# A second level of block products in the second projection, with softmax, attention and normalisation moved to other stages

## Chip, cores, metric

One core of one Trainium2 chip. The metric is the device time of one execution in microseconds; a kernel's time is the median of its runs. Ratios are the mean time of one kernel's fast runs over the mean of the other's fast runs of the same rounds, so they are not quite the ratio of the medians printed beside them. Every experiment was timed against the kernel before on the same chip in the same rounds, and across experiments I compare ratios, as the chips differ a little.

## The reference, cut to what matters

Input x is 128 x 64 x 512, float32. One layer, added to x:

```python
h = relu(layernorm(x))
# first graph attention: H = 4 heads, each 512 -> 512
Wh  = einsum('bnf,hfo->bhno', h, W_heads)
e   = leaky_relu(f1 + f2), masked by adj;  attn = softmax(e)
h   = elu(attn @ Wh)                      # 4 heads side by side: 2048 columns
# second graph attention: one head, 2048 -> 512
Wh2 = h @ W_out
out = elu(softmax(scores(Wh2)) @ Wh2)
# feed-forward and final norm
y   = relu(out @ w1 + b1) @ w2 + b2 + out
x   = x + layernorm(y) * ln_gamma + ln_beta
```

The 8192 rows are worked off in 16 groups of 512 rows. "Second projection" is `h @ W_out`.

## The kernel before

Each 512 x 512 product is cut into 2 x 2 blocks and done with seven block products in place of eight (`unit`). A block product of the second projection is four float32 matmuls of 256 columns per head (`product_n`). Its seven results are combined while they leave PSUM, the memory that TensorE writes to (an *eviction* is such a step out of PSUM): one VectorE addition, some ScalarE copies.

```python
    def unit(name, product, post, order):
        own = {1: 1, 2: 1, 5: 5, 3: 5, 6: 6, 7: 6, 4: 6}   # the PSUM bank of each product
        def after(p):
            if p in (1, 5, 6):
                ...
                if p == 6:
                    nc.vector.tensor_tensor(gb[6], gb[6], sb["s1"], ALU.add)
                nc.scalar.copy(sb[nm], gb[p])
                post(nm, sb[nm])
            ...
    def product_n(ms, blocks):
        ...
                    w, a = piece(ms[i], p), blocks(p, i)      # 256 KB of weights
                    for k in range(2):
                        for j in range(2):
                            nc.tensor.matmul(bk[:, j, :], a[:, k, ts(j, P)], w[:, k, :], ...)
```

The final norm, a tile of 128 rows at a time, was placed in the second stage, between the feed-forward products:

```python
        def finish(j):
            t = G * g + j
            xr = load(t, "xr")
            nc.gpsimd.tensor_tensor(xr, xr, bs, ALU.add)
            y = o[:, j]
            mean, rstd = norm_stats(y, "n2", t)     # ends with a GpSimd power operation
            nc.vector.scalar_tensor_tensor(y, y, mean, gs, ALU.subtract, ALU.mult)
            nc.vector.scalar_tensor_tensor(y, y, rstd, xr, ALU.mult, ALU.add)
            nc.sync.dma_start(out=of[ts(t, P), :], in_=y)
```

A group has two stages. In the **head stage** the first projection runs (products g_a) with the second attention of the previous group beside it (`stage_e`: scores, softmax, transposes, attention). In the **second stage** the second projection runs (g_b), then the feed-forward of the previous group (g_c, g_d), with the first attention of later groups beside it.

Of the kernel before, what the change touches and what calls it, by code (L numbers as in the profile page):

```python
# [18 lines left out]
AHEAD = 150  # L19


@with_exitstack
def gat_preln_kernel(
# [63 lines left out]
    mhalf = const.tile([P, 1], FP, name="mhalf")  # L87
# [4 lines left out]
    def load(t, name="x"):  # L92

        tl = wk.tile([P, F], FP, tag="x", name=f"{name}{t}", bufs=4)
        nc.sync.dma_start(out=tl, in_=xf[ts(t, P), :])
        return tl
# [47 lines left out]
    MT, TC = {}, {}  # L144
    DIRECT = {}

    def fetch(m):
        MT[m] = big.tile([P, KC, O], FP, tag=homes[m], name=f"pw{m}")
        queue = nc.scalar if m < H else nc.gpsimd
        queue.dma_start(out=MT[m], in_=mats[m].rearrange("(k p) o -> p k o", p=P))  # L150
# [13 lines left out]
    def turn_a():  # L164

        rows = H * 2 * KC
        pt = aux([P, rows], "pah")
        nc.tensor.transpose(pt, ah, ident[0:rows, 0:rows])
        aT = wk.tile([P, H, 2, KC], FP, tag="s1", name="aT")
        nc.scalar.copy(aT.rearrange("p h c o -> p (h c o)"), pt)  # L170
        return aT

    def fold_dve(m, ab):

        for k in range(KC):
            for c in range(2):
                junk = wk.tile([P, O], FP, tag="t", name=f"jk{c}_{m}_{k}")
# [21 lines left out]
    def weight_sums(m, after=None):  # L199
# [20 lines left out]
        TC[m] = [dram.tile([P, 2, 2, Q], FP, name=f"tc{m}_{i}") for i in range(2)]  # L220
# [19 lines left out]


    late = []
# [17 lines left out]
    def unit(name, product, post, order):  # L260
# [5 lines left out]
        def after(p):  # L266
            if p in (1, 5, 6):
                nm = {1: "s1", 5: "s5", 6: "t"}[p]
                sb[nm] = wk.tile([P, 2, T], FP, tag=nm, name=f"{nm}_{name}")
# [30 lines left out]
    def product_t(m, blocks):  # L300

        def product(p):
            def fn(bk, start):
                w, a = piece(m, p), blocks(p)
                for o in range(2):
                    for k in range(2):
                        nc.tensor.matmul(  # L307
# [6 lines left out]
    def product_n(ms, blocks):  # L314

        def product(p):
            def part(i):
                def fn(bk, start):
                    w, a = piece(ms[i], p), blocks(p, i)
                    for k in range(2):  # L320
                        for j in range(2):
                            nc.tensor.matmul(  # L322
# [17 lines left out]
    def norm_stats(src, tag, t):  # L340

        st = sm.tile([P, 6], FP, tag=tag + "st", name=f"{tag}st{t}")
        nc.vector.bn_stats(st, src)
        mv = sm.tile([P, 2], FP, tag=tag + "mv", name=f"{tag}mv{t}")
        nc.vector.bn_aggr(mv, st)
        ve = sm.tile([P, 1], FP, tag=tag + "ve", name=f"{tag}ve{t}")
        nc.vector.tensor_scalar(ve, mv[:, 1:2], EPS, None, ALU.add)  # L347
        rstd = sm.tile([P, 1], FP, tag=tag + "rs", name=f"{tag}rs{t}")
        nc.gpsimd.tensor_tensor(rstd, ve, mhalf, ALU.pow)
        return mv[:, 0:1], rstd  # L350

    def norm1(t):
        if t not in X:
            X[t] = load(t)
        mean, rstd = norm_stats(X[t], "n1", t)
        nb = sm.tile([P, 1], FP, tag="n1nb", name=f"n1nb{t}")
        nc.gpsimd.tensor_scalar(nb, mean, rstd, -1.0, ALU.mult, ALU.mult)
        HN[t] = big.tile([P, F], FP, tag="hn", name=f"hn{t}", bufs=G)
        nc.scalar.activation(HN[t], X.pop(t), AF.Relu, bias=nb, scale=rstd)
# [15 lines left out]
    def project_f(g):  # L375
# [15 lines left out]
        eng = nc.vector if g == 0 else nc.gpsimd  # L391
        eng.tensor_tensor(
# [65 lines left out]
    A1, E1, LAST = {}, {}, {}  # L458
# [4 lines left out]
    def transpose_weights(p):  # L463
        A = A1.pop(p)
        for j in range(2):
# [7 lines left out]
            AT[t] = big.tile([P, NB, H, N], FP, tag="at", name=f"at{t}", bufs=G)  # L473
# [6 lines left out]
    def stage_a(g):  # L480


        if g >= NG:
            return [], [], []
        p, r = 2 * g, 2 * g + 1

        def norms(p):
            norm1(2 * p)
            norm1(2 * p + 1)
            if p >= 2:  # L490
                prefetch(2 * p + 2)
                prefetch(2 * p + 3)

        def transposes(p):
# [3 lines left out]
        return (  # L498
            [lambda: norms(p), lambda: norms(r)],
            [  # L500
                lambda: transposes(p), lambda: transposes(r), nothing, lambda: project_f(g), nothing,
                lambda: (scores1(g), attn_weights(p)), nothing, lambda: attn_weights(r),
            ],
            [nothing, lambda: transpose_weights(p), nothing, nothing, lambda: transpose_weights(r)],
        )
# [4 lines left out]
    def attend1(g):  # L510
# [3 lines left out]
        def task(j, half):  # L514
# [6 lines left out]
            banks = [bank(f"pz{nm}_{t}_{b}") for b in range(NB)]  # L521
# [8 lines left out]
            for b in range(NB):  # L530
# [3 lines left out]
                if b == 0:  # L534
# [28 lines left out]
    def project1(g, h):  # L563
# [11 lines left out]
        def post(what, a, b=None, to=None):  # L575
# [8 lines left out]
            if what == "c21":  # L584
                nc.gpsimd.tensor_tensor(dst, dst, H1["22"][:, h], ALU.add)  # L585

# [15 lines left out]
    WH2 = {}  # L602

    def project2(g):
        slot = {1: "11", 2: "12", 3: "12", 4: "22", 5: "S1", 6: "11", 7: "S1"}
        h1 = dict(H1)
        wh = big.tile([P, G, FO], FP, tag="wh2", name=f"wh2_{g}")
        WH2[g] = wh

        def post(what, a, b=None, to=None):  # L610
            behind = {"s1": ("11", "S1", "11"), "s5": ("S1", "22", "11"), "c11": ("12", "12", "11")}
            if what in behind:
                dst, x0, x1 = (h1[n] for n in behind[what])
                for h in range(H):
                    nc.gpsimd.tensor_tensor(dst[:, h], x0[:, h], x1[:, h], ALU.subtract)  # L615
# [11 lines left out]
            f"b{g}", product_n(ms, lambda p, i: h1[slot[p]][:, i]), post, (1, 5, 6, 2, 7, 3, 4)  # L627
# [5 lines left out]
    def scores2(g, j):  # L633
# [3 lines left out]
        for c in range(2):  # L637
            junk = wk.tile([P, FO], FP, tag="elu", name=f"jf{g}_{j}_{c}", bufs=3)
            nc.vector.scalar_tensor_tensor(  # L639
                junk, WH2[g][:, j], 1.0, ao[:, c, :], ALU.mult, ALU.mult,  # L640
                accum_out=f[:, c, j:j + 1],
            )

# [27 lines left out]
    def attend2(g, j):  # L671
        pa = aux([P, FO], f"pa2_{g}_{j}")
        nc.tensor.matmul(pa, AT2[g][:, j, :], WH2[g][:, j, :], start=True, stop=True)  # L673
# [5 lines left out]
    def stage_e(g):  # L679

        gap = [lambda: None]
        score = [lambda j=j: scores2(g, j) for j in range(G)]
        attend = [lambda j=j: attend2(g, j) for j in range(G)]
        return (
            gap + score + [lambda: spread2(g)] + gap * 2 + [lambda: softmax2(g)] + gap * 5
            + [lambda: transpose_weights2(g)] + gap * 2 + attend[0:2] + gap + attend[2:4] + gap * 3
        )


    def feed_forward(g):  # L690
# [42 lines left out]
        def post2(what, a, b=None, to=None):  # L733
# [5 lines left out]
            eng = nc.vector if what[0] == "c" else nc.gpsimd  # L739
            eng.tensor_tensor(dst, a, dst, ALU.add)  # L740

        def finish(j):
            t = G * g + j
            xr = load(t, "xr")
            nc.gpsimd.tensor_tensor(xr, xr, bs, ALU.add)
            y = o[:, j]
            mean, rstd = norm_stats(y, "n2", t)
            nc.vector.scalar_tensor_tensor(y, y, mean, gs, ALU.subtract, ALU.mult)
            nc.vector.scalar_tensor_tensor(y, y, rstd, xr, ALU.mult, ALU.add)
            nc.sync.dma_start(out=of[ts(t, P), :], in_=y)  # L750

        f1 = unit(f"c{g}", product_t(M1, lambda p: bl[1][p]), post1, (1, 5, 6, 2, 3, 7, 4))
        f2 = unit(f"d{g}", product_n([M2], lambda p, i: bl[2][p]), post2, (1, 5, 6, 2, 3, 7, 4))
        return (
            [lambda j=j: transpose_out(j) for j in range(G)], f1 + f2,
            [lambda j=j: finish(j) for j in range(G)],
        )

    def mix(*lists):

        lists = [l for l in lists if l]
        keyed = [((i + 0.5) / len(l), n, fn) for n, l in enumerate(lists) for i, fn in enumerate(l)]
        return [fn for _, _, fn in sorted(keyed, key=lambda k: k[:2])]
# [4 lines left out]
    for t in range(G):  # L768
        norm1(t)
# [45 lines left out]
    for t in range(G, 2 * G):  # L815
        prefetch(t)
    for g in range(NG):
        if g >= 1:
            side = stage_e(g - 1)
        else:  # L820
            side = sum(stage_a(1), [])
# [73 lines left out]
```

## Time and profile before

| | kernel before |
|---|---|
| median of 3 runs | 2364.24 us (2363.18 to 2365.32) |
| profiled span | 2360.4 us |
| a steady group | 142.96 us |
| its head stage, first g_a to first g_b | 50.9 us |
| its second stage, from a full run of g_b to the next g_a | 89.2 us |
| TensorE busy | 98% |

The two stage lengths are worked out from start times in the TensorE timeline; a mixed stretch of some 3 us between them is in neither. I use them as "head" and "second".

The prediction shows the page's first lines and the steady stretches. What it does not show is TensorE's list of waits (columns: who waits for whom, us in total, times, longest). Its longest entries occur once each, in the start; two of them:

```profile
PE pzS L525 <- DVE z L537: 5.5, 1, 5.5
...
PE pab L158 <- DMA ar<-in_L_gnn_a_heads_dram: 5.4, 1, 5.4
```

Two VectorE groups by form, to be compared later (columns: busy us, mean ns of one, idle before it and what ended it). Both have two inputs in SBUF; the first is the score sum of the second attention, the second the last step of the final norm:

```profile
L639 DVE SCALAR_TENSOR_TENSOR jf<-wh,ao 128x512 f32<-128x512 f32 x128 | 94.3, 776 | 40.3 <-ACT wh L621 40.1
L749 DVE SCALAR_TENSOR_TENSOR o<-o,n2rs,xr 128x512 f32<-128x512 f32 x64 | 47.7, 767 | 0.8 <-POOL n2rs L349 0.8
```

### The profile page before, as it was taken

To read this page: it belongs to the slowest core of one execution; us is meant where nothing else is said; L and a number is where in the kernel's file an instruction comes from. 1 tells how busy PE (TensorE), PEld (TensorE's weight loads), DVE (VectorE), ACT (ScalarE), POOL (GpSimd) and SP (SyncE) were. 2 spreads that over 40 slices of the span, in tenths; PEclk is the share of its full clock that TensorE was granted. 3 is DMA by queue.
4 is the path that set the end of the run, shared out by engine and by line. 5 is a ranking of instruction groups with operands and counts; after the bars stand their busy time and mean duration, and the time that the engine had idled before them with its cause. 6 is when DMAs were issued, how large, how long until landed. Compare 5 with 4: busy or idle time off the path is not lost.

```text
span 2360.4 us, 32849 instructions
## 1 busy us (share of the span) xinstructions
PE 2317.9 (98%) x11805; PEld 1934.5 (82%) x11805; DVE 1265.5 (54%) x2210; ACT 911.0 (39%) x1623; POOL 1026.7 (43%) x917
## 2 busy tenths in 40 slices
PE   6989999999999999999999999999999999999997
PEld 4868787888878888787887878888788887878885
DVE  7625474554646556474554745556464563744527
ACT  2524425253352533425244251533525344251513
POOL 5664444416344353443524444253443534533333
PEclk7999999999999999999999999999999999999999
DMA  8545353444535445353444544435354453534443
GB/s 308 184 142 193 125 183 127 164 152 132 182 125 178 134 139 179 126 180 129 154 163 129 182 131 161 153 130 181 127 177 132 138 179 127 182 118 164 157 148 106
DMA packets 257809, 366.89 MB, mean 155 GB/s; under 512 B 22216, under 2 KB 145128, under 8 KB 257648
## 3 DMA queue, kind: packets, MB, share of 16 engines
q1 hardware_dynamic: 251024, 343.82, 43.9%
q0 software_dynamic: 4512, 16.78, 1.9%
q10 hardware_dynamic: 2112, 4.19, 0.5%
q8 instruction: 95, 1.56, 0.3%
q14 instruction: 66, 0.54, 0.1%
HBM read 337.45 MB, written 27.26 MB: 155 GB/s over the span
## 4 chain that ended last, share of the span: by engine, by line
PE 94%; DVE 2%; ACT 1%; POOL 1%; issue 0%; DMA 0%; DVEq 0%
PE g_b L322 33%; PE g_a L307 32%; PE g_c L307 8%; PE g_d L322 8%; PE pz L525 4%; PE pa L673 2%; PE pto L700 1%; PE pzS L525 1%; PE pth L371 1%; PE s1pt L472 1%; PE pf L381 1%; PE s1pe L406 1%; DMA x<-in_x_dram 0%; PE s2pt L667 0%; PE pwa L193 0%
## 5 line engine op out<-in xcount | busy, mean ns | idle before, releaser
L322 PE MATMUL g_b<-w,h 128*128 128x256 f32 x2560 | 598.1, 381 | 0.0
L322 PEld LDWEIGHTS g_b<-w,h 128*128 128x128 f32 x2560 | 480.5, 190 | 72.2 <-issue 10.1
L307 PE MATMUL g_a<-z,w 128*128 128x256 f32 x1520 | 361.0, 380 | 1.2 <-DVE g_a L581 0.7
L307 PE MATMUL g_a<-zs_z,w 128*128 128x256 f32 x1504 | 347.9, 379 | 0.0
L307 PEld LDWEIGHTS g_a<-z,w 128*128 128x128 f32 x1520 | 287.6, 190 | 57.9 <-issue 14.3
L307 PEld LDWEIGHTS g_a<-zs_z,w 128*128 128x128 f32 x1504 | 284.8, 190 | 50.5 <-issue 14.3
L322 PE MATMUL g_b<-w,hS 128*128 128x256 f32 x1024 | 243.5, 382 | 0.0
L585 POOL TENSOR_TENSOR hS<-hS,h 128x512 f32<-128x512 f32 x64 | 83.0, 1297 | 366.8 <-DVE hS L549 366.8
L547 ACT ACTIVATE exc<-g_a 128x512 f32<-128x512 f32 x256 | 152.3, 595 | 199.7 <-DVE g_a L581 119.6
L322 PEld LDWEIGHTS g_b<-w,hS 128*128 128x128 f32 x1024 | 191.4, 191 | 30.9 <-issue 6.7
L549 DVE SCALAR_TENSOR_TENSOR h<-exc,g_a 128x512 f32<-128x512 f32 x192 | 131.6, 686 | 136.3 <-ACT exc L548 136.2
L548 ACT ACTIVATE exc<-exc 128x512 f32<-128x512 f32 x256 | 161.6, 631 | 6.5
L615 POOL TENSOR_TENSOR h<-h,h 128x512 f32<-128x512 f32 x64 | 86.7, 1362 | 138.1 <-PE g_b L322 138.0
L332 POOL TENSOR_TENSOR zs_z<-zS,z 128x512 f32<-128x512 f32 x63 | 89.7, 1424 | 128.3 <-PE g_a L307 123.7
L615 POOL TENSOR_TENSOR h<-hS,h 128x512 f32<-128x512 f32 x64 | 81.1, 1268 | 142.4 <-PE g_b L322 142.4
L474 ACT COPY at<-s1pt 128x512 f32<-128x512 f32 x64 | 34.7, 588 | 279.8 <-PE s1pt L472 279.8
L307 PE MATMUL g_c<-ot,w 128*128 128x256 f32 x512 | 123.9, 385 | 0.8 <-DVE n2ve L347 0.8
L322 PE MATMUL g_d<-w,rt 128*128 128x256 f32 x512 | 121.5, 380 | 1.7 <-DVE o L740 1.0
L307 PE MATMUL g_a<-zS,w 128*128 128x256 f32 x496 | 117.2, 379 | 0.0
L639 DVE SCALAR_TENSOR_TENSOR jf<-wh,ao 128x512 f32<-128x512 f32 x128 | 94.3, 776 | 40.3 <-ACT wh L621 40.1
L333 POOL TENSOR_TENSOR zs_z<-z,zs_z 128x512 f32<-128x512 f32 x63 | 85.4, 1357 | 61.1 <-PE g_a L307 40.7
L307 PEld LDWEIGHTS g_c<-ot,w 128*128 128x128 f32 x512 | 93.9, 190 | 21.8 <-issue 9.3
(159 smaller groups left out, 3535.6 us busy)
## 6 DMA issues: line engine op xcount, KB each, us to landing
w<-tc SPq DMA_DIRECT2D x632, 256.0 KB, 2.6
w<-in_L_gnn_W_heads_dram SPq DMA_DIRECT2D x192, 256.0 KB, 2.7
w<-in_L_gnn_W_out_dram SPq DMA_DIRECT2D x192, 256.0 KB, 2.7
w<-in_L_gnn_w_dram SPq DMA_DIRECT2D x96, 256.0 KB, 2.7
x<-in_x_dram SPq DMA_DIRECT2D x66, 256.0 KB, 3.6
xr<-in_x_dram SPq DMA_DIRECT2D x64, 256.0 KB, 2.8
out_dram<-o SPq DMA_DIRECT2D x64, 256.0 KB, 2.1
tc<-pt POOLq DMA_DIRECT2D x20, 512.0 KB, 5.6
```

Of the source, the lines that this page charges most:

```text
L307: nc.tensor.matmul(bk[:, o, :], w[:, k, ts(o, P)], a[:, k, :], start=start and o == 0 and k == 0, stop=k == 1, skip_group_check=True,)
L322: nc.tensor.matmul(bk[:, j, :], a[:, k, ts(j, P)], w[:, k, :], start=start and k == 0 and j == 0, stop=i == len(ms) - 1 and k == 1, skip_g ...
L332: eng.tensor_tensor(s2, s1, a11, ALU.subtract)
L333: eng.tensor_tensor(s4, a12, s2, ALU.subtract)
L525: nc.tensor.matmul(banks[b][:, c, :].rearrange("p (h n) -> p h n", h=H), src[rows, off + c * P:off + (c + 1) * P], at[rows, b], start=True ...
L547: nc.scalar.activation(ex, src, AF.Relu, scale=-1.0)
L548: nc.scalar.activation(ex, ex, AF.Exp, scale=-1.0)
L549: nc.vector.scalar_tensor_tensor(dst, ex, -1.0, src, ALU.add, ALU.max)
L585: nc.gpsimd.tensor_tensor(dst, dst, H1["22"][:, h], ALU.add)
L615: nc.gpsimd.tensor_tensor(dst[:, h], x0[:, h], x1[:, h], ALU.subtract)
L639: nc.vector.scalar_tensor_tensor(junk, WH2[g][:, j], 1.0, ao[:, c, :], ALU.mult, ALU.mult, accum_out=f[:, c, j:j + 1],)
L673: nc.tensor.matmul(pa, AT2[g][:, j, :], WH2[g][:, j, :], start=True, stop=True)
```

## The change

The intent is to take work from TensorE: each of the seven products of the second projection is cut once more, into seven of quarter size (7 x 7 x 4 heads = 196 matmuls of 128 columns for 7 x 16 = 112 of 256). This runs in groups 4 to 15, the *deep* groups below; groups 1 to 4 prepare the summed weights. Softmax and first attention of the next group move into the second stage, half of the final norm moves on into the next head stage (`last`), and "not urgent" operations are tied behind the last issued matmul (`behind_pe`) so that they do not take their engine's place from an eviction. Its core:

```diff
+DEEP = 4
+    def behind_pe(ins):            # a dependency on the last issued matmul
+        if "pe" in LAST:
+            tc.add_manual_dep(ins.ins, LAST["pe"].ins.name, ...)
+    def project2_deep(g):
+        def quarter_sum(p, j):     # 21 a group, 128x512, two SBUF inputs
+            eng = nc.gpsimd if p in (3, 7, 4) else nc.vector
+            ...
+        def inner(r, eng):         # recombines the inner level: 5 operations, twice a group
+            behind_pe(eng.tensor_tensor(...)); eng.tensor_tensor(...) ...
+        def part(p, half, j):
+                w, x = small_piece(p, j), operand(p, j)
+                for h in range(H):
+                    LAST["pe"] = nc.tensor.matmul(bk[:, place[j][1]], x[:, h], w[:, h], ...)
+                ...
+                        if p == 7:
+                            inner(0, nc.gpsimd)
+                        if p == 4:
+                            inner(1, nc.gpsimd)
+        def fin_load(j):
+            xr[j] = load(t, "xr")
+            nc.gpsimd.tensor_tensor(xr[j], xr[j], bs, ALU.add)
+        def fin_stats(j, gate=True):      # two tiles at a time; one power operation
+        def fin_out(j, gate=True):        # the two scalar_tensor_tensor, then the output transfer
-            [lambda j=j: finish(j) for j in range(G)],
+            (fin_load, fin_stats, fin_out),
     # second stage of group g (a position is a share of the stage's steps):
+            tasks += [(0.60 + 0.08 * j, lambda j=j: fin_load(j)) for j in range(G)]
+            tasks += [(0.84, lambda: fin_stats(0))]
+            tasks += [(0.93 + 0.03 * j, lambda j=j: fin_out(j)) for j in range(2)]
     # head stage of group g + 1:
+            last = [(0.03, lambda f=fin_stats: f(2))]
+            last += [(0.09 + 0.03 * j, lambda j=j, f=fin_out: f(2 + j)) for j in range(2)]
     # second attention, in the head stage:
+            [(0.14 + 0.06 * j, lambda j=j: scores2(g, j)) for j in range(G)]
+            + [(0.36, lambda: spread2(g)), (0.44, lambda: softmax2(g))]
+            + [(0.64, lambda: transpose_weights2(g))]
+            + [(0.72 + 0.06 * j, lambda j=j: attend2(g, j)) for j in range(G)]
```

Also: buffers are taken from others to make room, and the copies of the first attention move from VectorE to ScalarE.

## The prediction

> **What bounds the kernel now.** I read the page first, then the busy time by stretch, the chain of waits in order of time, the groups by form, the TensorE timeline and the packet records. Page: span, busy time, chain.
>
> ```profile
> span 2360.4 us, 32849 instructions
> PE 2317.9 (98%) x11805; PEld 1934.5 (82%) x11805; DVE 1265.5 (54%) x2210; ACT 911.0 (39%) x1623; POOL 1026.7 (43%) x917
> ...
> PE 94%; DVE 2%; ACT 1%; POOL 1%; issue 0%; DMA 0%; DVEq 0%
> PE g_b L322 33%; PE g_a L307 32%; PE g_c L307 8%; PE g_d L322 8%; PE pz L525 4%; PE pa L673 2%; PE pto L700 1%; PE pzS L525 1%; PE pth L371 1%; PE s1pt L472 1%; PE pf L381 1%; PE s1pe L406 1%; DMA x<-in_x_dram 0%; PE s2pt L667 0%; PE pwa L1
> ```
>
> TensorE is busy for 98% and carries 94% of the chain. The stretches say the same for one steady group: head stage (products g_a), then second stage (g_b, the second projection, with g_c and g_d, the feed-forward, between). Columns: window, length, then busy us of each engine, granted clock, DMA share, GB/s.
>
> ```profile
> 1191.45:1242.21 50.76, 50.76 (x230) 43.21 (x230) 27.21 (x52) 28.31 (x51) 11.69 (x9) 1.00 0.45 148
> 1242.21:1334.41 92.20, 92.20 (x506) 76.51 (x505) 50.81 (x82) 28.40 (x51) 48.90 (x44) 1.00 0.46 151
> sum 142.96, PE 142.96 PEld 119.73 DVE 78.02 ACT 56.72 POOL 60.59; mean PE 71.48 PEld 59.86 DVE 39.01 ACT 28.36 POOL 30.30
> ```
>
> PE busy equals the length in both: no gap in 143 us, at full clock. Groups 1 to 14 all repeat at 142.96 us. So in steady state only fewer or shorter TensorE instructions count; moving softmax, norm or copies about earns nothing there. All idle is at the ends:
>
> ```profile
> 0.00:50.00 50.00, 30.91 (x137) 20.66 (x139) 35.20 (x100) 11.46 (x20) 32.65 (x47) 0.74 0.96 346
> 50.00:100.00 50.00, 48.54 (x296) 40.72 (x293) 31.58 (x58) 28.27 (x50) 32.65 (x34) 0.99 0.40 131
> 100.00:150.00 50.00, 43.82 (x218) 33.66 (x217) 21.41 (x33) 20.22 (x35) 32.69 (x35) 0.93 0.60 203
> 150.00:190.73 40.73, 39.02 (x234) 33.41 (x233) 16.04 (x31) 7.54 (x14) 19.80 (x20) 1.00 0.43 143
> ...
> 2290.00:2360.40 70.40, 56.34 (x251) 44.80 (x249) 48.37 (x90) 21.24 (x41) 23.45 (x20) 0.96 0.32 112
> ```
>
> That is 19 + 1.5 + 6 + 2 us at the start and 14 us at the end.
>
> **What the Trainium skill says.** The question is how fast pairs of weight load and 128-column matmul run.
> (1) "TensorE: Matmul & The Clock Gate", section "LDWEIGHTS": a load takes its columns over 1.2 GHz, so 107 ns for 128. The trace agrees. In the start, at clock 0.50, pwa is 32 pairs of a full 128x128 f32 load with a matmul of only two columns, which leaves the load as the bound:
>
> ```profile
> 28.44 6.99 PE L193 MATMUL pwa<-aT,wT 128*128 128x2 f32 x32
> ...
> 28.60:35.40 6.80, 6.80 (x33) 6.74 (x32) 5.11 (x17) 1.17 (x2) 6.75 (x9) 0.50 1.01 358
> ```
>
> About 213 ns a pair at half clock, so 107 at full.
> (2) Same page, "Back-to-back issue gap": spacing follows the streamed columns plus 2.5 ns, but in real streams of load and matmul at 128 columns the page has some 81 ns where the formula gives 56. So pairs can be slower than either half. The trace for 256 columns in f32: 24 in 5.18 us, 216 ns each, so half of it, about 108 plus some ns, for 128.
> (3) "SBUF — State Buffer", "Who interferes with whom": a VectorE operation with two SBUF inputs contends with a GpSimd one that reads SBUF. The trace agrees: zs_o (two SBUF inputs) takes 1.2 to 1.65 us where g_a plus a copy (one PSUM input) takes 0.70.
> (4) "DMA: Bandwidth & Descriptors", "Specifications": rows from 512 B up keep line rate. The packet records: 1,024 B in 51 ns, 2,048 B in 95, 512 B in 27 (only 32 of those); times 16 engines that is 324, 343 and 303 GB/s.
>
> **The change part by part.**
> *Two levels in the second projection, groups 4 to 15 (12 of 16).* Now: 7 products x 4 heads x 4 matmuls x 2 (each f32 matmul is two instructions in the trace: 3584 g_b for 16 groups) = 224 instructions of 256 columns, 224 x 0.216 = 48.4 us a group. After: 7 x 7 x 4 heads x 2 = 392 of 128 columns. The nearest in the trace are the transposes, each with its own 128x128 load:
>
> ```profile
> 1327.31 1.04 PE L472 MATMUL s1pt<-ident,s1A 128*128 128x128 f32 x8
> 1328.19 0.60 PE L322 MATMUL g_b<-w,h 128*128 128x256 f32 x2
> ```
>
> Eight in 0.88 us: 110 ns, with the ordinary load of the next g_b hidden behind the last of them. A transpose's load is shorter (140 ns recorded against 190), so this alone does not settle it; with the 107 of pwa I take 109.5. 392 x 0.1095 = 42.9 us, **5.4 us less a group, 65 us in all**, from a stage on the path throughout. The load then ends only 2 ns before it is needed.
> *Other engines, per deep group.* Quarter sums: 21 of 128x512, 12 on VectorE (some 1.3 us each from zs_o, 16 us), 9 on GpSimd (1.36 each, 12 us); the inner combinations add 2 x 5 GpSimd operations of 256 or 512 columns, some 11 us. Away from VectorE: 8 copies of pz (5.5 us, now ScalarE); to it: the R product (1.3) and two additions of post2 (1.4). GpSimd's power operations are halved in number. In the second stage, norm statistics, score sums and half of the final norm also move to the head. I get VectorE some 56 of 87 us there and 36 of 51 in the head, GpSimd some 55 of 87. None becomes a bound on average; beside TensorE, so 0 us.
> *Moves.* Softmax and attention for group g+1 into the second stage of g, norm into the head: PE work unchanged, 0 us in steady state; less work in front of group 1, perhaps 2 us less idle at the start. Tying operations to the last issued product keeps evictions ahead: 0 us.
> *Transfers.* 49 pieces of 256 KB for 28: 21 more, so 103 for 82 a group, 27.0 MB in 137.5 us = 196 GB/s for 150. 21 of the 49 come in rows of 512 B. In packet time 39.5 us of all engines instead of 21.9, so a share of 0.46 becomes about 0.60. Alone, a piece is used up in 0.88 us and takes 0.76 to 0.86; between feed-forward products there is more time, and 11 buffers are ahead. Hidden.
> *Preparation, groups 1 to 4.* 14 sets of sums (4 GpSimd operations, 1 MB moved) in buffers that the next stage wants: one or two short waits, +2 us.
> *End.* After the last product now come GpSimd's five inner operations (5.4 us) before the scores of the last two tiles. Now the last g_b ends at 2292.6 and s2pe stands at 2297.9, s2pt at 2303.8 just after a wait. The filler is the same, so +5 us.
> *Sum.* 2364.2 - 65 - 2 + 2 + 5 + 3 (some 0.2 us per group of new waits, a guess) = **2307 us**.
>
> **Rivals.**
> *A. The pairs run slower than 109.5 ns.* For: (2) above, and load and matmul both stand at 107 to 109, so there is no slack. Against: pwa, and the g_b load behind a transpose. At 116 ns the saving is 2.9 us a group: 2337. From 123.4 on there is none, and the rest leaves about 2372.
> *B. New waits of TensorE.* The eviction of six bank halves, the quarter sums feeding the next product, and operations held back until a product has run all share in-order queues; one late operation stops the rest. Two banks are free at most. For: more work on VectorE and GpSimd, contending as in (3). Against: both under 70%, sums a product ahead. 2 us a deep group makes 2331.
> *C. Transfers.* For: stretches at near 300 GB/s and the smaller rows. Against: 346 GB/s at the start. 1.5 us a deep group makes 2325.
> *D. Better ends.* Softmax and attention a stage later could take 5 more us out of the first 190: 2302.
>
> **Range and chances.** 2% is at 2317, which leaves me 10 us of slack on a saving of 65. A, B and C all go upward, and I give each one in six to eight of costing those 10 us; D is worth a few us the other way. So a predicted time of 2307, a range of 2290 to 2334, faster by over 2% at 0.70, within 2% at 0.26, slower at 0.04.
>
> **What would show it.** The first projection stays at 216 ns. Deep g_b: 392 instructions of 128 columns a group, starts 109 to 110 ns apart; 116 or more is A. Groups 0 to 3 repeat at about 143 us, 4 to 14 at about 137.5, with PE busy equal to the length; idle of PE in front of g_b or g_a released by VectorE, GpSimd or ScalarE is B, by a DMA C. DMA share about 0.60. The end longer by some 5 us, waiting for the inner sums. The prediction is wrong if the spacing is over 114 ns or deep groups show over 1 us of waits.

## More of the kernel before

Differences of ratios are turned into microseconds with 2364 us.

Note for later: product 7 accumulates on bank 6, so it can start only when VectorE's addition and ScalarE's copy after product 6 are done.

## The result, and the profile after

The changed kernel takes **2482.82 us** (2481.64 to 2487.11, 3 runs), a ratio of 1.0506 [1.0482, 1.053]: 5% slower. The prediction was wrong. Page of the kernel after: span, busy time, chain:

```profile
span 2485.3 us, 38062 instructions
PE 2318.2 (93%) x13821; PEld 1988.5 (80%) x13821; DVE 1527.9 (61%) x2321; ACT 988.0 (40%) x1803; POOL 1381.5 (56%) x1172
...
PE 56%; DVE 21%; POOL 12%; issue 7%; ACT 4%; DMA 1%; DVEq 0%; SPq 0%; POOLq 0%; ACTq 0%
```

TensorE's share of the chain fell from 94% to 56%; VectorE and GpSimd now hold a third of it, though neither is busy for more than 61%. The same columns as in the prediction, for the two stages of group 8:

```profile
1237.16:1301.20 64.04, 55.77 (x246) 46.03 (x245) 49.53 (x84) 32.69 (x58) 38.55 (x35) 0.97 0.50 156
1301.20:1388.03 86.83, 85.86 (x661) 77.42 (x660) 49.15 (x63) 29.48 (x57) 48.97 (x38) 1.00 0.68 198
```

The second stage is shorter than before, as was hoped. The head stage is 13 us longer, with 8.3 us in which TensorE does nothing, and its clock is below full. (The cut of this stretch lies a few instructions later than before's, so lengths are better taken from first g_a to first g_b: 62.0 us for 50.9.) The waits of TensorE:

```profile
PE g_a L365 <- POOL xr L926: 51.4, 11, 4.7
PE s2pe L836 <- DVE s2dg L827: 21.1, 13, 3.7
PE s2pt L846 <- DVE s2A L528: 17.3, 13, 2.9
PE s1pe L484 <- DVE R L470: 16.7, 12, 6.3
```

The largest stands once in the head of each of groups 5 to 15, those that follow a deep second stage. The next two are in most heads; s1pe is one wait of 6.25 us in the start and 0.95 us in the second stage of each of groups 4 to 14. None of them names a transfer.

**The accounting.** The spans differ by 124.9 us. By stretches, cut at each group's first g_a:

| stretch | before | after | difference |
|---|---|---|---|
| start and group 0 | 190.6 | 188.0 | -2.6 |
| groups 1 to 3 (old products, moved tasks, preparation) | 428.9 | 449.2 | +20.3 |
| group 4 | 142.96 | 147.15 | +4.2 |
| groups 5 to 14 (nine at 142.96 and the last at 137.0 before; some 150.87 each after) | 1423.7 | 1508.8 | +85.1 |
| group 15 and end | 174.3 | 192.2 | +17.9 |

Groups 1 to 3 have none of the new products and still lose 6.8 us each on average. So the loss is not only a matter of the products.

**The products themselves** did what was predicted. A piece of the chain in time order (start, length, what):

```profile
1320.81 2.68 PE g_b L761 x24
```

That is 111.7 ns a pair of load and matmul (predicted 109.5; no gain from 123.4 on). 392 x 0.1117 = 43.8 us for 48.4: 4.6 us less a group.

**Where the head stage stands.** Four engines around TensorE's largest wait, in the order in which it builds up (start, length, instruction, idle before it). GpSimd first:

```profile
1241.64 1.26 POOL L745 TENSOR_TENSOR wh<-wh 128x512 f32<-128x512 f32 x1
...
1246.13 0.72 POOL L751 TENSOR_TENSOR wh<-wh 128x256 f32<-128x256 f32 x1
1246.81 0.70 POOL L420 TENSOR_TENSOR n2r<-n2v,mhalf 128x2 f32<-128x2 f32 x1
```

The `wh` lines are `inner(1)`, 5.2 us in all. The power operation n2r, 0.70 us of work, had its input n2v at 1242.93 (the end of VectorE's L418 in the timeline) and stood 3.9 us behind them in GpSimd's queue. VectorE and ScalarE:

```profile
1243.10 1.15 DVE L936 SCALAR_TENSOR_TENSOR o<-o,n2m,gs 128x512 f32<-128x512 f32 x1
1247.55 1.74 DVE L939 SCALAR_TENSOR_TENSOR o<-o,n2r,xr 128x512 f32<-128x512 f32 x1 [3.30 <-POOL n2r L420]
1249.21 0.69 DVE L330 TENSOR_TENSOR g_a<-g_a,s_a 128x512 f32<-128x512 f32 x1
...
1249.93 0.59 ACT L331 COPY t_a<-g_a 128x512 f32<-128x512 f32 x1 [8.48 <-DVE g_a L330]
```

The final norm's last step waits 3.30 us for n2r, and **behind it in VectorE's queue stands L330, the eviction of product 6**, which does not need n2r at all. Then TensorE:

```profile
1244.07 1.89 PE L365 MATMUL g_a<-zs_z,w 128*128 128x256 f32 x8
1250.62 3.05 PE L365 MATMUL g_a<-zs_z,w 128*128 128x256 f32 x8 [4.66 <-POOL xr L926]
1253.46 2.53 PE L365 MATMUL g_a<-z,w 128*128 128x256 f32 x8
```

Product 7 starts at 1250.62, 0.10 us after ScalarE's t_a ended. The profile puts the wait down to GpSimd's xr, an addition whose result no matmul reads. Releasers are inferred from semaphore events, and another event fell at about the same time. The kernel's structure (bank 6) and the 0.10 us name t_a, and through it L330. Product 7's own operand is not it: GpSimd's last zs sum before `inner(1)` ended at 1241.68. The distance is the better proof. Product 7 starts 1.41 us after L330 does here, and 1.40 to 1.42 us after it in a head of each of e11 to e15 below, whether the profile names GpSimd's xr, its zs or "issue" as the releaser. And the wait is paid twice. Eight matmuls should start 1.73 us apart from the next eight; after the wait they take 1253.46 - 1250.62 = 2.84 and then 2.37 us, 1.75 us more in sum: the clock has dropped, which is the 0.97 of the stretch.

The other waits of this head stage are 0.74 (g_a), 1.34 (s2pe) and 1.20 us (s2pt). With 4.66 and the 1.75 that makes 9.7 of the 11.1 us.

**Contention beside it.** The same two VectorE groups as before:

```profile
L815 DVE SCALAR_TENSOR_TENSOR jf<-wh,ao 128x512 f32<-128x512 f32 x128 | 151.4, 1210 | 10.4 <-POOL wh L751 10.4
L939 DVE SCALAR_TENSOR_TENSOR o<-o,n2r,xr 128x512 f32<-128x512 f32 x64 | 94.3, 1474 | 38.7 <-POOL n2r L420 36.3
```

The same work takes 1210 ns for 776 and 1474 for 767. That GpSimd beside it is the reason shows in this head:

```profile
1250.88 1.75 DVE L815 SCALAR_TENSOR_TENSOR jf<-wh,ao 128x512 f32<-128x512 f32 x1
...
1257.11 0.68 DVE L815 SCALAR_TENSOR_TENSOR jf<-wh,ao 128x512 f32<-128x512 f32 x1
```

The first runs beside GpSimd's xr addition and zs sum, the second while GpSimd stands idle (1257.11 to 1258.71, waiting for xr's transfer).

### The profile page after: what moved, and what is told of

The parts are those of the page before. It is cut to its first block, busy times and chain, and to the rows that moved or that the text cites. A ratio compares the mean times of both kernels' runs of the same rounds, so it can differ in the third digit from the quotient of the medians.

```text
span 2485.3 us, 38062 instructions
## 1 busy us (share of the span) xinstructions
PE 2318.2 (93%) x13821; PEld 1988.5 (80%) x13821; DVE 1527.9 (61%) x2321; ACT 988.0 (40%) x1803; POOL 1381.5 (56%) x1172
## 3 DMA queue, kind: packets, MB, share of 16 engines
q1 hardware_dynamic: 370928, 416.72, 55.5%
## 4 chain that ended last, share of the span: by engine, by line
PE 56%; DVE 21%; POOL 12%; issue 7%; ACT 4%; DMA 1%; DVEq 0%; SPq 0%; POOLq 0%; ACTq 0%
PE g_b L761 15%; PE g_a L365 10%; PE g_b L380 8%; PE g_c L365 7%; PE g_d L380 6%; DVE jf L815 4%; PE pz L593 4%; DVE g_a L649 2%; POOL zs_z L391 2%; POOL zs_z L392 2%; DVE h L617 1%; DVE o L939 1%; PE pa L852 1%; POOL zs_z L390 1%; POOL wh L750 1%
## 5 line engine op out<-in xcount | busy, mean ns | idle before, releaser
L365 PE MATMUL g_a<-zs_z,w 128*128 128x256 f32 x1504 | 374.5, 397 | 51.4 <-POOL xr L926 51.4
L365 PEld LDWEIGHTS g_a<-zs_z,w 128*128 128x128 f32 x1504 | 299.1, 200 | 118.4 <-POOL xr L926 55.5
L761 PE MATMUL g_b<-wq,q 128*128 128x128 f32 x2016 | 265.0, 277 | 4.2 <-POOL q L707 2.1
L761 PEld LDWEIGHTS g_b<-wq,q 128*128 128x128 f32 x2016 | 248.0, 192 | 15.0 <-issue 7.3
L761 PE MATMUL g_b<-wq,h 128*128 128x128 f32 x1920 | 251.9, 278 | 0.0
L761 PEld LDWEIGHTS g_b<-wq,h 128*128 128x128 f32 x1920 | 235.1, 192 | 16.0 <-issue 7.7
L603 ACT COPY z<-pz 128x512 f32<-128x512 f32 x186 | 100.2, 589 | 233.7 <-PE pz L593 233.6
L815 DVE SCALAR_TENSOR_TENSOR jf<-wh,ao 128x512 f32<-128x512 f32 x128 | 151.4, 1210 | 10.4 <-POOL wh L751 10.4
L380 PE MATMUL g_b<-w,h 128*128 128x256 f32 x640 | 152.8, 383 | 0.0
L380 PEld LDWEIGHTS g_b<-w,h 128*128 128x128 f32 x640 | 117.7, 190 | 21.0 <-issue 5.3
L685 POOL TENSOR_TENSOR hS<-h,h 128x512 f32<-128x512 f32 x64 | 85.9, 1364 | 84.8 <-PE g_b L761 55.7
L380 PE MATMUL g_d<-w,rt 128*128 128x256 f32 x512 | 123.4, 384 | 2.1 <-DVE o L919 1.0
L365 PE MATMUL g_c<-ot,w 128*128 128x256 f32 x512 | 123.4, 384 | 0.9 <-DVE ot L890 0.9
L926 POOL TENSOR_TENSOR xr<-xr,bs 128x512 f32<-128x512 f32 x64 | 97.9, 1537 | 37.2 <-DMA xr<-in_x_dram 35.1
```

What stands on the lines that cost most here:

```text
L365: LAST["pe"] = nc.tensor.matmul(bk[:, o, :], w[:, k, ts(o, P)], a[:, k, :], start=start and o == 0 and k == 0, stop=k == 1, skip_group_che ...
L380: LAST["pe"] = nc.tensor.matmul(bk[:, j, :], a[:, k, ts(j, P)], w[:, k, :], start=start and k == 0 and j == 0, stop=i == len(ms) - 1 and k ...
L603: nc.scalar.copy(dst, srcv)
L685: nc.gpsimd.tensor_tensor(dst[:, h], x0[:, h], x1[:, h], ALU.subtract)
L761: LAST["pe"] = nc.tensor.matmul(bk[:, place[j][1]], x[:, h], w[:, h], start=first and h == 0, stop=h == H - 1, skip_group_check=True,)
L815: ins = nc.vector.scalar_tensor_tensor(junk.rearrange("p (c v o) -> p c v o", c=2, v=2), WH2[g][j], 1.0, ao[:, c, :].rearrange("p (c v o) ...
```

## The experiments

Theory at this point, called the **queue theory**: urgent evictions stand behind the moved operations in the in-order queues of VectorE and GpSimd, where the head and second stage meet; the moved norm and the inner sums bring this about, and the products are innocent. Rivals: the **two-level products** cost the time by themselves (quarter sums, contention, buffers); the **ties** to the last issued product hold operations back.

### Which part of the change costs the time

**e1_nodeep**: the change without two-level products.

```diff
-DEEP = 4
+DEEP = 16
```

> The changed kernel with the two-level scheme switched off (DEEP = 16: second projection, preparation and GpSimd inner sums as in the kernel before), all moves and ties kept. Theory 1 (the loss is in the head stage: VectorE's queue there is filled at its start with final norm and score sums, TensorE waits for its evictions, the clock falls after long waits; the two-level products themselves save): still much slower than before, groups of 147 to 150 us, about 2440 to 2460 us. Theory 2 (the two-level scheme costs the time, by its extra GpSimd, VectorE and transfer work): about 2365 us.

Measured 2435.28 us, 1.0302 [1.0286, 1.0317]. More than half of the loss is there without a single new product: heads of 54.5 to 57.5 us (group 1: 51.4), second stages of 89.5, about as before. TensorE waits 38 us in 14 waits of 1.9 to 3.0 us for VectorE's addition in the head. So the moved tasks cost 71 us alone, and the two-level scheme adds 48 although it saves 55 on TensorE.

**e2_late**: the last half of the final norm later in the head stage.

```diff
-            last = [(0.03, lambda f=fin_stats: f(2))]
-            last += [(0.09 + 0.03 * j, lambda j=j, f=fin_out: f(2 + j)) for j in range(2)]
+            last = [(0.46, lambda f=fin_stats: f(2))]
+            last += [(0.50 + 0.03 * j, lambda j=j, f=fin_out: f(2 + j)) for j in range(2)]
```

> The changed kernel with one edit: the second half of the final norm (statistics of two tiles and their output) stands at 0.46 to 0.53 of the head stage instead of 0.03 to 0.12. Theory 1: the wait of 4.7 us before the seventh product of the first head, VectorE standing behind GpSimd's power operation, goes away with the half-speed clock after it: 5 to 7 us off each of 12 groups, about 2400 us. Theory 2: no change, about 2480 us.

Measured 2431.03 us, 1.0282 [1.0265, 1.0299]. A change of position alone, with the same work, takes back 53 us; deep heads fall from 62 to between 55.5 and 57.2. But the wait moves: s2pt now waits 41.1 us in all for the second softmax (17.3 in the kernel after). So this place is not free either; no other in the head was tried.

**e3_notie**: no ties.

```diff
-        if "pe" in LAST:
+        if False:
```

> The changed kernel with the ties to the last issued product left out (the dependency alone is dropped; it guards no data). If the ties are what keeps score sums and norm in the crowded first third of the head stage, the waits there spread out: 2400 us or less. If they do what they are meant for, holding back what is not urgent, evictions come later without them and it is slower than 2480 us.

Measured 2474.6 us, 1.0469 [1.0453, 1.0485]. Without ties it is 9 us faster, so they are not what costs 120. But that is the difference of two larger effects, by the two profiles: without ties start and group 0 take 18 us more (206.4 for 188.0) and groups 1 to 4 22 us more (their heads reach 64 to 67 us; TensorE waits 74.1 us in all for ScalarE's copy s_a), while groups 5 to 14 take 43 us less (heads of 57 us) and the rest 11 less. The rival was half right: in the deep groups the ties do cost.

**e4_deeponly**: the kernel before with the two-level scheme alone: `project2_deep`, its preparation, its buffers (8 weight buffers for 11, one s1, s5 and t each for two, the room in the products' tile), the PSUM banks of the first attention in deep groups, and the order of the feed-forward products; old placement of all tasks. **e5_buffers** is the same with `DEEP = 16`, so the buffers without the scheme.

> The kernel before with the two-level scheme alone (groups 4 to 15, preparation in groups 1 to 4; ring of 8 pieces for 11 and single buffers for the saved products, to make room; copies of pz from the small banks in deep groups), in the order of the kernel before, without moves and ties. Theory 1: the products save about 4.6 us in 12 groups, the end costs some 5: 2315 to 2330 us. Theory 2: slower than 2364 us, groups of 148 us or more.

> Control for e4: the same kernel with the two-level scheme off (DEEP = 16), so only its smaller ring and single buffers for the saved products are left. If the two-level work itself made the waits of e4, this is near the kernel before, 2364 to 2400 us. If the buffers made them (groups 1 and 3 of e4 have no two-level product and were slow too), it is above 2480 us, and e4 says little of the scheme.

e4 measured 2594.05 us, 1.0973 [1.0954, 1.0991]; e5 2371.17 us, 1.0025 [1.0009, 1.0042]. The buffers by themselves are excluded: e5 repeats 50.9 and 89.2 us. In e4 deep heads are 53.5 to 55.2 us and deep second stages 100 to 103 (88.7 in group 14). Its largest wait of TensorE:

```profile
PE g_d L379 <- DVE o L916: 70.0, 23, 8.0
```

In the old placement the scheme crowds VectorE's queue in the *second* stage instead (g_d's evictions). Groups 1 and 3, which only prepare, have long second stages too (100.6 and 103.2). So the scheme does not fit the old placement as it stands. e4 does not separate the scheme's own cost from the cost of a placement that does not fit it, and I draw no more from it.

**e6_finsecond**: the change with the whole final norm back in the second stage. **e7_fs_nodeep**: the same with `DEEP = 16`.

```diff
-            tasks += [(0.54 + 0.058 * i, fn) for i, fn in enumerate(ff[7:])]
+            tasks += [(0.54 + 0.045 * i, fn) for i, fn in enumerate(ff[7:])]
-            tasks += [(0.60 + 0.08 * j, lambda j=j: fin_load(j)) for j in range(G)]
-            tasks += [(0.84, lambda: fin_stats(0))]
-            tasks += [(0.93 + 0.03 * j, lambda j=j: fin_out(j)) for j in range(2)]
-            last = [...]
+            tasks += [(0.50 + 0.08 * j, lambda j=j: fin_load(j)) for j in range(G)]
+            tasks += [(0.75 + 0.11 * j, lambda j=j: fin_stats(2 * j)) for j in range(2)]
+            tasks += [((0.79, 0.83, 0.90, 0.94)[j], lambda j=j: fin_out(j)) for j in range(4)]
```

> The changed kernel with the whole final norm at the end of the second stage (feed-forward products 0.045 apart for 0.058, statistics at 0.75 and 0.86, outputs from 0.79 to 0.94) and none of it in the head stage. Theory 1: heads of 52 to 54 us for 62, second stages still near 86: 2330 to 2365 us. Theory 2 (two-level work on GpSimd and VectorE at the stage's border is what delays): heads stay above 58 us, 2430 us or more.

> e6 with the two-level scheme off. It gives the scheme's worth in a head stage that is not crowded: theory 1 has heads of 51 to 53 us and second stages of 89.5, about 2370 to 2385 us, so e6 is faster by 30 us or more. Theory 2: at or below 2365 us and faster than e6.

e6 measured 2441.85 us, 1.0315 [1.0291, 1.0339]; e7 2369.22 us, 1.0016 [1.0001, 1.0031]. With e1 and the kernel after that is a table of two by two:

| ratio | half of the final norm in the head stage | all of it in the second stage |
|---|---|---|
| two-level from group 4 | 1.0506 (after) | 1.0315 (e6) |
| no two-level | 1.0302 (e1) | 1.0016 (e7) |

The norm in the head costs 68 us without the scheme, and in e7 a steady stretch is TensorE-bound again, busy for its whole length (window of 143 us, same columns as above):

```profile
1055.00:1198.00 143.00, 143.00 (x735) 119.46 (x734) 76.06 (x130) 60.16 (x109) 52.88 (x44) 1.00 0.49 151
```

So without the scheme softmax and attention in the second stage, the ties, the pairing of statistics, the change's buffers and the move of copies cost nothing to speak of; among the moves, **the norm in the head is the one that costs**. But my theory falls short in the right column: with the norm out of the head, the scheme still costs 2.99%, 71 us. e6 heads are still 58 to 60 us, now with this wait:

```profile
PE s2pe L836 <- DVE s2dg L827: 47.6, 11, 5.0
```

Both parts load the head, and the loads do not add up (the two alone would make 1.060, the change has 1.0506); they share something. Part of it: "second stage" is where e6 issues the norm. With the scheme, its last steps still run in the first microseconds of the head, as the timelines of e11 and e12 below show.

### What the two-level scheme puts into the head stage

**e8_fs_scores**: e6 with the first attention's scores and transposes later in the second stage, to take away TensorE's wait for VectorE's product R (s1pe).

```diff
-            (0.20, lambda: (scores1(g), attn_weights(p))), (0.26, lambda: attn_weights(r)),
-            (0.42, lambda: transpose_weights(p)), (0.50, lambda: transpose_weights(r)),
+            (0.24, lambda: (scores1(g), attn_weights(p))), (0.30, lambda: attn_weights(r)),
+            (0.45, lambda: transpose_weights(p)), (0.52, lambda: transpose_weights(r)),
```

> e6 with the attention scores at 0.24 and 0.30 of the second stage for 0.20 and 0.26, and the transposes after them at 0.45 and 0.52. In deep groups of the changed kernel TensorE waited some 1.4 us for VectorE's R product ahead of the scores. If that wait is only the position, 10 to 17 us less than e6; if the later softmax then stops the transposes, no gain.

Measured 2428.85 us, 1.0274 [1.0256, 1.0293]. The s1pe waits fall from 12.7 to 2.2 us and the second stage to 84.9; the wait of 47.6 us in the head stays. So this is a small wait of its own, removed for some 10 us. The chain in e8's head runs through the inner sums to the score sums, their spread (s2dg), which s2pe waits for:

```profile
1223.73 1.24 POOL wh L745
...
1229.29 3.43 DVE jf L815 x4
...
1237.27 1.43 DVE s2dg L827
```

**e9_after_inner** and **e10_inner**: from this chain, `inner(1)` on VectorE, in the kernel after (e9) and in e8 (e10).

```diff
-                            inner(1, nc.gpsimd)
+                            inner(1, nc.vector)
```

> The changed kernel with the last inner sums (second half of the rows) on VectorE in place of GpSimd, nothing else. If GpSimd's queue at the stage's border is what delays (the inner sums stand there behind six additions for the next heads, and VectorE waits for them and for the power operation behind them), 4 to 7 us less in each of 12 groups, 2400 to 2435 us. If VectorE itself is the bound of the head stage, moving work to it costs: 2480 us or more.

> e8 with the same edit as e9: in a head stage without the final norm. In e8 the score sums of the last two tiles began 17 us after the last product, 5.6 of it GpSimd's inner sums behind its other work, and TensorE waited 4.3 us a group for what follows. Queue theory: that wait is mostly gone, heads of 52 to 55 us, 2350 to 2385 us. VectorE-bound theory: no gain over 2429 us.

e9 measured 2458.34 us, 1.0391 [1.0375, 1.0406]: 27 us back, where 48 or more were expected. e10 measured 2423.11 us, 1.0247 [1.0225, 1.0268]: 6 us against e8, within the intervals, and its heads stay at 58.9. The queue theory had 2350 to 2385 there: a miss. The wait for s2dg is gone, but 55.7 us of waits in front of g_a, 12 times, have come in its place.

**e11_inner_shift**: e10 with the second softmax and attention later in the head.

```diff
-            + [(0.36, lambda: spread2(g)), (0.44, lambda: softmax2(g))]
-            + [(0.64, lambda: transpose_weights2(g))]
-            + [(0.72 + 0.06 * j, lambda j=j: attend2(g, j)) for j in range(G)]
+            + [(0.42, lambda: spread2(g)), (0.53, lambda: softmax2(g))]
+            + [(0.72, lambda: transpose_weights2(g))]
+            + [(0.79 + 0.05 * j, lambda j=j: attend2(g, j)) for j in range(G)]
```

> e10 with the second attention's steps later in the head stage (0.42 and 0.53 for 0.36 and 0.44, transposes 0.72, products from 0.79). If what is left are only positions on TensorE that come too early, heads of 51 to 53 us, 2320 to 2350 us. If VectorE and GpSimd are too busy in the head stage at any position, no more than 5 us less than e10.

Measured 2422.57 us, 1.0237 [1.0222, 1.0253]: no change in time, and none of the 70 us or more that was hoped for. Taking one wait away in the head only lets the next one end last. Its timelines show which. GpSimd, then VectorE, then TensorE, in one head stage of e11:

```profile
1207.10 1.77 POOL L926 TENSOR_TENSOR xr<-xr,bs 128x512 f32<-128x512 f32 x1 [1.38 <-DMA xr<-in_x_dram]
...
1213.58 0.70 POOL L420 TENSOR_TENSOR n2r<-n2v,mhalf 128x2 f32<-128x2 f32 x1
```

```profile
1214.31 1.75 DVE L939 SCALAR_TENSOR_TENSOR o<-o,n2r,xr 128x512 f32<-128x512 f32 x1 [6.57 <-POOL n2r L420]
...
1224.87 0.69 DVE L330 TENSOR_TENSOR g_a<-g_a,s_a 128x512 f32<-128x512 f32 x1
```

```profile
1226.29 3.75 PE L365 MATMUL g_a<-zs_z,w 128*128 128x256 f32 x8 [4.97 <-issue]
```

It is the same pattern as in the kernel after, with other members. GpSimd waits for xr's transfer, then does `inner(0)` and the sums zs, and only then n2r. VectorE stands 6.57 us for it in the last step of the final norm, and everything behind it runs late, down to L330 and TensorE's wait of 4.97 us. The output transfer behind L939 holds up the transfer queue as well: nothing is issued there from 1206.98 to 1216.09.

### Taking both things out of GpSimd's queue

Two things stand in front of n2r: `inner(0)`, and the xr addition that is not tied and waits for its data. Each was removed alone and both together.

**e14_shift_tie** (e11 with the tie), **e15_shift_inner0** (e11 with the other half of the inner sums on VectorE), **e12_inner_both** (both), and **e13_after_tie** (the tie alone in the kernel after). The two edits:

```diff
-            nc.gpsimd.tensor_tensor(xr[j], xr[j], bs, ALU.add)
+            behind_pe(nc.gpsimd.tensor_tensor(xr[j], xr[j], bs, ALU.add))
```

```diff
-                            inner(0, nc.gpsimd)
+                            inner(0, nc.vector)
```

> e11 with both sets of inner sums on VectorE and the additions to the residual rows tied to the last product, so that they do not run early in the head stage, beside the score sums. If contention of GpSimd and VectorE is what stretches the score sums (0.73 to 1.75 us each), those come back to about 0.8 us and this is faster than e11 by 5 us or more, 2310 to 2335 us. If not, it is within 5 us of e11.

> The changed kernel with one edit: the additions to the residual rows tied to the last issued product, like the change's other operations that are not urgent. Chain theory (GpSimd stands at such an addition, hoisted ahead of the inner sums and waiting for its own transfer, so its power operation comes late, VectorE stands at the norm's output that needs it, and evictions, output transfers and weight loads stand behind): 15 to 40 us less than the changed kernel, 2440 to 2468 us. If those additions are only load, not a blockage: within 10 us of 2483.

> e11 with the tie of e13 alone, the first inner sums still on GpSimd. Together with e15 it splits the 68 us from e11 to e12. Chain theory: the tie is the larger part, 2360 to 2390 us. Load theory (GpSimd's 5 us of inner sums in front of the power operation): above 2400 us.

> e11 with both inner sums on VectorE, without the tie, the other half of e12. Chain theory: the hoisted additions still stop GpSimd, above 2385 us. Load theory: near e12, 2355 to 2370 us.

| | median us | ratio [95%] | deep heads us | L939's waits for n2r, us in total |
|---|---|---|---|---|
| e11 | 2422.57 | 1.0237 [1.0222, 1.0253] | 57.3 to 59.9 | 65.0 |
| e14, tie | 2406.49 | 1.0184 [1.017, 1.0198] | 56.5 to 58.1 | 27.6 |
| e15, inner(0) | 2400.46 | 1.0155 [1.0141, 1.0169] | 54.6 to 57.9 | 29.2 |
| e12, both | 2354.73 | 0.9955 [0.9939, 0.9972] | 52.5 | none listed |
| e13, after with tie | 2441.23 | 1.0328 [1.0313, 1.0342] | 58.0 to 59.6 | 36.3 |

The tie alone gives 13 us, `inner(0)` alone 19 (e14 expected the tie to be the larger part: a miss), both 67. It is not an amount of work on VectorE: e12 has five more VectorE instructions a group than e11 and e14, and is faster by 67 and 54 us. But it is not queue position alone either. The same eight VectorE operations stand between n2r and L330 in all four; from their first (L939) to L330, in e14:

```profile
1201.97 1.75 DVE L939 SCALAR_TENSOR_TENSOR o<-o,n2r,xr 128x512 f32<-128x512 f32 x1 [2.50 <-POOL n2r L420]
...
1206.99 1.75 DVE L745 TENSOR_TENSOR wh<-wh 128x512 f32<-128x512 f32 x1
...
1213.61 0.68 DVE L330 TENSOR_TENSOR g_a<-g_a,s_a 128x512 f32<-128x512 f32 x1
```

and in e15:

```profile
1217.03 1.75 DVE L939 SCALAR_TENSOR_TENSOR o<-o,n2r,xr 128x512 f32<-128x512 f32 x1 [1.82 <-POOL n2r L420]
...
1221.16 0.68 DVE L745 TENSOR_TENSOR wh<-wh 128x512 f32<-128x512 f32 x1
...
1223.74 0.69 DVE L330 TENSOR_TENSOR g_a<-g_a,s_a 128x512 f32<-128x512 f32 x1
```

| group 8's head | L939 starts, from first g_a | L939 to L330 | GpSimd busy, first g_a to L330 | TensorE's wait before product 7 | clock of the head |
|---|---|---|---|---|---|
| e11 | 1.80 us late | 10.56 us | 90% | 4.97 us | 0.94 |
| e14, tie | 0.77 us early | 11.64 us | 94% | 3.47 us | 0.94 |
| e15, inner(0) | 3.93 us late | 6.71 us | 64% | 3.25 us | 0.94 |
| e12, both | 0.79 us late | 7.48 us | 60% | 0.88 us | 1.00 |

Two things make L330 late: n2r comes late (queue order: in e15 GpSimd waits 7.50 us for an xr transfer ahead of it, which the tie cures), and the eight operations take longer beside a busy GpSimd (contention, which taking `inner(0)` off GpSimd largely cures). Either edit leaves the other. And the clock adds to what both give: after the three longer waits the next sixteen matmuls take 2.6 to 3.0 us more than 3.46, after the wait of 0.88 us only 0.07. The head stage of e12, from GpSimd to TensorE:

```profile
1188.50 0.69 POOL L420 TENSOR_TENSOR n2r<-n2v,mhalf 128x2 f32<-128x2 f32 x1 [0.44 <-DVE n2m L419]
```

```profile
1189.45 1.57 DVE L939 SCALAR_TENSOR_TENSOR o<-o,n2r,xr 128x512 f32<-128x512 f32 x1
...
1196.93 0.69 DVE L330 TENSOR_TENSOR g_a<-g_a,s_a 128x512 f32<-128x512 f32 x1
```

```profile
1198.34 1.97 PE L365 MATMUL g_a<-zs_z,w 128*128 128x256 f32 x8 [0.88 <-issue]
```

GpSimd now waits for n2r's input (0.44 us) and no longer the other way round, L939 goes without a wait, and of TensorE's wait 0.88 us is left. The group repeats at 139.98 us for 142.96 before, with a second stage of 83.7.

e13 has the time that its chain theory expected, but not by that chain: the tie in the kernel after gives 42 us and shortens the head from 62.0 to some 58, while L939's waits for n2r stay at 36.3 us and TensorE's largest wait stays too (54.7 us in 11 waits, for 51.4; `inner(1)` still stands in front of n2r). What went is contention later in the head: with the xr additions out of the way, the score sums (L815) take 769 ns for 1210, and TensorE's waits for s2dg (21.1 us in the kernel after) are gone. So n2r is one link by which GpSimd reaches TensorE, and contention is another.

**e16_polish**, with 5 rounds: e12, with the last group's quarter sums on VectorE and the transposes and attention of the second softmax a little later.

```diff
-            eng = nc.gpsimd if p in (3, 7, 4) else nc.vector
+            eng = nc.gpsimd if p in (3, 7, 4) and g < NG - 1 else nc.vector
-            + [(0.72, lambda: transpose_weights2(g))]
-            + [(0.79 + 0.05 * j, lambda j=j: attend2(g, j)) for j in range(G)]
+            + [(0.76, lambda: transpose_weights2(g))]
+            + [(0.82 + 0.045 * j, lambda j=j: attend2(g, j)) for j in range(G)]
```

> e12 with all quarter sums of the last group on VectorE (TensorE waited 1.7 and 2.1 us for them there, with no other work between its products) and the second attention's transposes at 0.76 and products from 0.82 (waits of 0.8 to 1.8 us in groups 1 to 4, with the half-speed clock after them). 5 to 10 us less than e12: 2345 to 2350 us, 0.6 to 0.8% below the kernel before.

Measured 2347.74 us, 0.9935 [0.9921, 0.9948]: the fastest of all, 0.65% faster than the kernel before (clear of noise; under 2%); by the two ratios (0.9935 / 1.0506) its time is 0.946 of the changed kernel's. Its page:

```profile
PE 2276.1 (97%) x13821; PEld 1965.7 (84%) x13821; DVE 1573.2 (67%) x2450; ACT 986.8 (42%) x1803; POOL 1221.7 (52%) x1043
...
PE 85%; DVE 5%; POOL 3%; ACT 2%; issue 2%; DMA 1%; SPq 0%; DVEq 0%; POOLq 0%; ACTq 0%
```

TensorE is back at 97% with VectorE busier than in the kernel after (67% for 61%). VectorE's busy share had nothing to say about what was wrong.

## Why the prediction was wrong

The step that failed is the one on the other engines: **"None becomes a bound on average; beside TensorE, so 0 us"**, and with it the term **"3 (some 0.2 us per group of new waits, a guess)"**. The first half of that sentence is true, and its "so" is false. In the second stage the averages even came out lower than predicted: VectorE 49 of 87 us (56), GpSimd 49 (55). In the head VectorE has 49.5 of 64 us for 36 of 51, partly because contention makes its operations longer, and still a quarter of the time free. But TensorE waits for one operation behind others, and an average shows neither what stands in front of it nor how long that takes there. In a deep group the waits are 7.9 us in the head and the dropped clock 1.75 us more, some 50 times the guess.

- **Products.** Right in kind: 111.7 ns a pair for 109.5, 4.6 us less a group for 5.4, so 55 us for 65 over 12 groups. Rival A (116 ns and more) did not come true. The second stage fell by 3.6 us of these 4.6 (85.9 for 89.5 in the groups without the scheme); the other 1.0 is the wait of 0.95 us before s1pe. (The 1.4 us in e8's expectation is 16.7 us over 12 waits; it takes in the one of 6.25 us in the start.)
- **Moves, "0 us in steady state".** Wrong: 1.0302 without any new product (e1). Softmax and attention in the second stage were free (e7). The norm in the head was not. I had looked at it as TensorE work, which it does not have, and had not asked in whose queue it stands ahead of an eviction.
- **"Tying operations to the last issued product keeps evictions ahead: 0 us."** Wrong for the kernel as it stood: the GpSimd addition of xr was left untied, and tying it gives 42 us (e13). The ties that there were are worth 9 us the wrong way on the whole (e3).
- **Transfers, "hidden".** Right: over the whole of group 8 the DMA share is 0.61 (0.60 predicted) at 180 GB/s, which in 150.9 us is 27.2 MB for the 27.0 worked out, and no large wait of TensorE names one. Rival C did not come true on TensorE. An indirect part did: xr's transfer keeps GpSimd waiting.
- **Start, -2 us.** -2.6. **Preparation, +2 us.** Too low: groups 1 to 3 lose 20.3 us, and 11.3 in e1, which lacks only the preparation there. So it costs some 9 us in these groups, and the norm most of the rest.
- **End, +5 us.** +17.9 with group 15, of which 9.5 are its head stage (60.4 us for 50.9).
- **Rival B** was the right one and named the mechanism (in-order queues, "one late operation stops the rest"). It was sized at 2 us a deep group and measured 11 in the head, and it was given one chance in six to eight. It was also tied to the deep groups, while groups 1 to 3 lost 6.8 us each. Its "Against" was again the averages ("both under 70%").
- **Readings.** "Groups 1 to 14 all repeat at 142.96 us" holds for 1 to 13; group 14 took 137.0 before. The zs_o figures under (3) compare different operations; the pair of L815 above is the comparison that shows contention.

**What stays open.** Contention and queue order are told apart in the heads of e11 to e15, not for the loss of the kernel after as a whole. Contention alone does not make it: e7 has no loss, with 978 ns for the score sums and 1261 for the norm's last step. e16 repeats at 140.18 us against 143.19 in e7: 3.0 of the 4.6 us that the products save arrive; 1.1 of the missing 1.6 stand in the head (52.5 for 51.4), the rest was not traced. The end of the kernel after was not studied by itself.

## What to carry to other kernels

When TensorE is the bound and work is moved to the other engines, do not ask how busy they are; ask for each eviction that TensorE waits for what stands in front of it in its engine's queue, for each of those, what *it* waits for on a third engine, and how long it takes beside what that engine then does. Here a 0.70 us operation behind 5 us of others on GpSimd had a part in a TensorE wait of 4.66 us, through an instruction on VectorE that has nothing to do with TensorE, and the clock then took its share on top. When two such causes meet, removing one shows little; test them together before dropping either.

## What the Trainium skill lacked or had wrong

- "TensorE: Matmul & The Clock Gate", "Back-to-back issue gap": for streams of load and matmul at 128 columns it gives some 81 ns, without a figure for float32. Here float32 pairs ran at 111.7 ns (24 in 2.68 us), close to the 107 ns for the load alone that its section "LDWEIGHTS" gives for 128 columns (an estimate from its 1.2 GHz).
- "SBUF — State Buffer", "Who interferes with whom": it says that a VectorE operation with two SBUF inputs contends with a GpSimd one that reads SBUF; of sizes it has two ratios, without the operations that they belong to. Here the mean of a 128x512 scalar_tensor_tensor rose from 776 to 1210 ns (jf) and from 767 to 1474 ns (L939, o); single ones of jf took 0.68 us alone and 1.75 beside GpSimd.
- I found no page that gives a duration for a power operation on GpSimd: means of 0.71 us on 128x2 in the kernel after, and of 0.56 to 0.87 us on 128x1 in the two kernels, so the second column did not set it.
